# First image of a convolution-plus-attention kernel: diagonal products in short runs between the keys, mean products placed among them, the first norm summed by products, the vectors' transfers first

## The chip, the cores and the metric

The kernel runs on one core of a Trainium2 chip. Its time is the device time of one execution in microseconds. Before the change four runs took 3025.23, 3026.17, 3026.61 and 3026.94 us; the median is 3026.39 us. One further execution was profiled, and every time inside the kernel below is from that execution, counted from the start of its span. PE is the engine for matrix products, DVE the vector engine, ACT the scalar engine, POOL the GpSimd engine; SP only issues transfers.

## What is computed

The input is a batch of 4 images of 384 channels and 48 x 48 points, all float32. Cut to what matters:

```python
x_flat  = x.reshape(B, C, N).transpose(0, 2, 1)              # N = 2304 points
local   = depthwise_conv_7x7(x, conv_w) * inv + shift        # batch norm folded in
x_norm  = layernorm(x_flat, ln_gamma, ln_beta)               # over the 384 channels
q, k, v = split(x_norm @ qkv_w.T + qkv_b)                    # 8 heads of 48
q       = q + heads(layernorm(local_flat, ln_gamma, ln_beta))
out     = softmax(q @ k.T * 48 ** -0.5) @ v
y       = x_flat + out @ proj_w.T + proj_b
```

## The kernel before, in words

**Tiling.** An image is cut into 6 chunks of 8 image rows, 384 points each (`G`), numbered g; all images together have 24 chunks, numbered t. Channels lie on 128 partitions in `CC` = 3 groups c. Tensors come packed: group c holds two heads at partitions 0 and 64 and a third of the last two heads in the 16 partitions behind each, so a load of one tensor (`load_packed`) is four transfers.

**Per image.** `keys_values` (L423) makes keys and values of one chunk. It is a generator of three steps, each of six products of 128 x 128 by 128 x 384 (a float32 product shows in the profile as two instructions): value blocks 0 and 1; value block 2 and key group 0; key groups 1 and 2. ACT moves the results out of PSUM; for keys it adds `qkb`, the projection's bias joined with what the norm's beta gives (`shift_rows` makes that by products with beta, a row of 384 numbers for each of queries 0, keys 1 and values 2).

**Per chunk of queries** a pass of 12 slots follows (`NSLOT`). A slot makes six score tiles (L649), lets ACT take the exponential (L653), and weighs the values with the six tiles of the slot before (L664). Into these slots the rest is laid: the next chunk's 7 x 7 convolution, its norm, its query projection, the last chunk's output projection.

**The convolution.** One tap of one channel group is one DVE instruction (L240), 147 for a chunk. `conv_ops(t)` yields after each. A planner (L263 to L302) gives each half slot a weight and deals the 147 instructions of chunk t+1 over the half slots up to the first norm slot of chunk t (`norm_slots`, L281: 7 and 10 for t = 0). For the first chunk of all, ten of the 49 taps (`PE_TAPS`) go to PE instead, as products with diagonal matrices: ACT makes 30 diagonals (L250) from the identity and the taps, PE runs ten products per group (L256), and `add_products` adds the result to the DVE's accumulator.

**The norm.** In the first image DVE adds the three channel groups (`chunk_sum`, L313 and L314), PE spreads the mean over all partitions by one product with a constant matrix (`spread_mean`, L320), DVE subtracts it (`centre`, L324), ACT squares (L328), DVE sums, PE spreads again, ACT takes the inverse root in three instructions (L335 to L337), DVE corrects it (`newton`, L403 to L405) and multiplies (L738; for the convolution's result L531, in `query_end`). During the slots another form is used: `sum_out` sends the sums through DRAM, and `centre_by`, `variance`, `few_root` and `few_newton` finish on 12 columns.

**The first image's start** (L684 to L750) is an order written out by hand: PE, DVE and ACT run their instructions as written. So does SP in the section of loads (L117 to L196). After that section a scheduler places SP's and POOL's transfers among the others. The vectors are loaded as `norms` (batch norm and layer norm) and `taps_in`, scaled into `natural`, and sent piece by piece into the packed layout `vec` by 14 transfers (L162), by turns from ACT's and POOL's queues. `taps` and `diagonals` need `vec`. In the loads' section SP issues, after the vectors and the first slab (the 11 image rows that the first chunk's convolution reads): `w_v`, `staged[1]` (key weights), the chunk `xn` 1, `staged[0]` (query weights), chunks 2 to 5, `w_o`. The next slab's load belongs to the first convolution instruction and so comes behind them, and then the bias: `row` is written to DRAM (`bias<-row`, L709) and read back as `columns` (four transfers).

PSUM has one bank `m` for means, one bank `sums`, and three double banks `r` in a ring.

## Time and profile before

| | |
|---|---|
| median of 4 runs | 3026.39 us |
| profiled execution, its own time | 3026.74 us |
| its span | 3024.5 us |
| PE busy | 2980.4 us, 99% |
| DVE busy | 2305.5 us, 76% |
| ACT busy | 1560.8 us, 52% |
| first product of the whole run | 14.14 us |
| first scores of the first chunk (L649) | 151.23 us |
| first scores of the second chunk | 259.58 us |

The span is the profiled time from the first to the last instruction; 2.24 us of the execution's own time lie outside it. The slices of the page cut the span into 40 equal parts of 75.6 us, so the first image's start is the first two of them. A wait is shown in brackets with the instruction or transfer that ended it. The granted clock is 1.00 at full speed.

### The profile page before, as it was taken

The page shows a single profiled execution, that of the slowest core. Times are in us where ns is not written, and L with a number is a line of the kernel's source. Part 1 is how long each engine was busy: PE and PEld are TensorE (multiplying, and loading weights), DVE is VectorE, ACT ScalarE, POOL GpSimd, SP SyncE. Part 2 cuts the span into 40 slices and gives each one's busy share as a digit, 9 for nine tenths or more (in the row PEclk, how much of TensorE's full clock was granted, in tenths as well). Part 3 has the DMA queues.
Part 4 walks back from the last instruction along what each step waited for, and adds up shares of the span by engine and source line. Part 5 has one row for each costly group of instructions (what it writes and reads, how often), then busy time and mean ns, then how long its engine had stood idle before and what let it go on. Part 6 is the DMA issues. An engine that isn't in the chain of part 4 may idle for free.

```text
span 3024.5 us, 42309 instructions
## 1 busy us (share of the span) xinstructions
PE 2980.4 (99%) x15686; PEld 1357.6 (45%) x15686; DVE 2305.5 (76%) x4569; ACT 1560.8 (52%) x2385; POOL 19.0 (1%) x61
## 2 busy tenths in 40 slices
PE   6999999999999999999999999999999999999998
PEld 3544444444454444444455444444445444444443
DVE  6899989978765899888765888987876488788411
ACT  3354555555435555555534555555552555555553
POOL 1000000000000000000000000000000000000000
PEclk9999999999999999999999999999999999999999
DMA  6111111111101211111110111012010111100001
GB/s 115 25 25 28 34 34 34 31 39 37 27 25 30 47 33 30 36 30 38 29 33 23 33 39 42 22 34 48 25 28 24 27 27 33 25 27 19 17 26 29
DMA packets 98618, 98.89 MB, mean 33 GB/s; under 512 B 43617, under 2 KB 89185, under 8 KB 98402
## 3 DMA queue, kind: packets, MB, share of 16 engines
q1 hardware_dynamic: 97010, 95.42, 14.2%
q8 instruction: 125, 2.05, 0.3%
q10 hardware_dynamic: 752, 0.63, 0.1%
q14 instruction: 91, 0.75, 0.1%
q0 software_dynamic: 640, 0.05, 0.0%
HBM read 70.24 MB, written 15.25 MB: 28 GB/s over the span
## 4 chain that ended last, share of the span: by engine, by line
PE 93%; DVE 6%; DMA 0%; ACT 0%; issue 0%; SPq 0%; DVEq 0%; ACTq 0%
PE r L649 38%; PE o L664 37%; PE m L411 10%; PE r L411 8%; DVE acc L240 4%; DMA vec<-natural 0%; PE m L320 0%; PE r L256 0%; DVE sum L314 0%; PE o L256 0%; PE r L861 0%; DVE sum L313 0%; DVE xn L738 0%; DVE xn L324 0%; DMA taps_in<-in_conv_w_dram 0%
## 5 line engine op out<-in xcount | busy, mean ns | idle before, releaser
L653 ACT ACTIVATE pt<-r 128x768 f32<-128x768 f32 x1728 | 1276.6, 812 | 1168.0 <-PE o L664 738.2
L240 DVE SCALAR_TENSOR_TENSOR acc<-slab,vec,acc 128x368 f32<-128x368 f32 (+8 forms) x3429 | 1735.9, 583 | 7.7 <-DMA vec<-natural 7.7
L664 PE MATMUL o<-pt,v 128*49 128x384 f32 x6912 | 1173.8, 489 | 0.0
L649 PE MATMUL r<-q,k 48*128 48x384 f32 x5184 | 910.4, 497 | 4.1 <-DVE q L533 4.1
L664 PEld LDWEIGHTS o<-pt,v 128*49 128x49 f32 x6912 | 425.8, 124 | 709.0 <-issue 681.5
L649 PEld LDWEIGHTS r<-q,k 48*128 48x128 f32 x5184 | 441.1, 186 | 472.2 <-ACT pt L653 224.8
L649 PE MATMUL r<-qt,kt 48*128 48x384 f32 x1728 | 300.7, 493 | 1.3 <-ACT pt L653 1.3
L627 DVE SCALAR_TENSOR_TENSOR xr<-m,pb,xr 128x384 f32<-128x384 f32 x69 | 42.5, 615 | 281.8 <-PE m L411 281.8
L649 PEld LDWEIGHTS r<-qt,kt 48*128 48x128 f32 x1728 | 150.4, 185 | 151.3 <-ACT pt L653 69.1
L411 PE MATMUL m<-xn,w_qk 128*128 128x384 f32 x414 | 152.0, 503 | 0.0
L411 PE MATMUL m<-ao,w_o 128*128 128x384 f32 x414 | 152.0, 503 | 0.0
L411 PE MATMUL r<-xn,w_qk 128*128 128x384 f32 x450 | 149.3, 486 | 0.7 <-ACT q L525 0.7
L411 PE MATMUL r<-w_v,xn 128*128 128x384 f32 x432 | 147.3, 494 | 0.0
L313 DVE TENSOR_TENSOR sum<-sq 128x384 f32<-128x384 f32 x48 | 26.7, 555 | 113.2 <-ACT sq L328 113.1
L411 PEld LDWEIGHTS r<-xn,w_qk 128*128 128x128 f32 x450 | 85.4, 190 | 60.6 <-ACT q L525 1.3
L411 PEld LDWEIGHTS r<-w_v,xn 128*128 128x128 f32 x432 | 83.4, 194 | 60.0 <-issue 4.9
L411 PEld LDWEIGHTS m<-xn,w_qk 128*128 128x128 f32 x414 | 73.0, 189 | 74.2 <-issue 27.8
L411 PEld LDWEIGHTS m<-ao,w_o 128*128 128x128 f32 x414 | 73.0, 189 | 74.2 <-issue 14.2
L581 DVE RECIPROCAL rd<-rd 128x24 f32<-128x24 f32 (+2 forms) x25 | 7.5, 301 | 128.6 <-DMA rd<-den 128.6
L451 ACT COPY v<-r 128x384 f32<-128x384 f32 x72 | 32.2, 481 | 126.0 <-PE r L411 126.0
L447 ACT ACTIVATE k<-r,qkb 128x384 f32<-128x384 f32 x72 | 39.4, 581 | 68.4 <-PE r L411 68.4
L564 ACT COPY ao<-o 49x384 f32<-49x384 f32 x141 | 66.6, 473 | 1.7
(113 smaller groups left out, 813.8 us busy)
## 6 DMA issues: line engine op xcount, KB each, us to landing
xr<-in_x_dram SPq DMA_DIRECT2D x24, 576.0 KB
out_dram<-xr SPq DMA_DIRECT2D x72, 192.0 KB
slab<-in_x_dram SPq DMA_DIRECT2D x32, 378.0 KB
rb<-rden SPq DMA_DIRECT2D x48, 216.0 KB
xn<-in_x_dram SPq DMA_DIRECT2D x46, 216.0 KB
slab<-in_x_dram SPq DMA_DIRECT2D x16, 297.0 KB
slab<-in_x_dram SPq DMA_DIRECT2D x32, 126.0 KB
kt<-k SPq DMA_DIRECT2D x144, 24.0 KB
```

Of the source, the lines that this page charges most:

```text
L240: nc.vector.scalar_tensor_tensor(dst, src, weight, dst, ALU.mult, ALU.add)
L313: nc.vector.tensor_add(s, src[:, 0, :], src[:, 1, :])
L411: nc.tensor.matmul(dst, lhsT=weights(c), rhs=src(c), start=c == 0, stop=c == CC - 1)
L447: nc.scalar.activation(k[:, u, :], r[:, j, :G], AF.Identity, bias=qkb[:, 1, u : u + 1])
L451: nc.scalar.copy(v[:, u + NB, :, 0:HD], r[:, j, :C].rearrange("p (h d) -> p h d", d=HD))
L564: nc.scalar.copy(dst[r : r + HA], sums[r : r + HA, :G])
L581: nc.vector.reciprocal(rd, rd)
L627: nc.vector.scalar_tensor_tensor(xr[:, co, :], m, pb[:, co : co + 1], xr[:, co, :], ALU.add, ALU.add)
L649: nc.tensor.matmul(r[:, j, :G], lhsT=kk[:, blk * P : (blk + 1) * P], rhs=qq, start=True, stop=True)
L653: nc.scalar.activation(pt, r[:, :, :G], AF.Exp, scale=SCALE)
L664: nc.tensor.matmul(sums[r : r + HA, :G], lhsT=values[t // NG, kb // NB][:, kb % NB, 2 * p + j, :], rhs=pt[:, j, :], start=kb == 0, stop=kb ...
```

## The change

The change touches the start of the run, the first image's keys and values, and the pass of the very first chunk. The vectors: the layer-norm vector and the taps are issued from ACT, the first chunk of x from SP behind the slab, POOL makes its constants first, and POOL issues nine of the 14 transfers of `vec` and ACT five. POOL's instructions in the loads' section now run as written. The diagonals are made in four portions, and the 30 products run in portions of 3, 4, 3 and then 5, all into the bank `sums`. The sums over channels of the first chunk's norm are made by three products each (`spread_sum`). The rows of the bias go out in two parts: those of keys and values before the first keys, read back by `key_bias`, that of the queries later, read back by `query_bias`. In the loop over chunks the first step of the keys comes ahead of the next chunk's mean, and the taps are dealt anew (4, 4, 3, 8). In the very first pass the norm's slots are 8 and 10, and its norm uses `chunk_sum`, `spread_mean`, `centre` and `newton`.

```diff
-    def load_x(b, g, queue=nc.sync):
+    def load_x(b, g):
         t = big.tile([P, CC, G], F32, tag=f"xn{g}", name=f"xn{b}_{g}")
-        load_packed(t, x[b, :, g * G : (g + 1) * G], queue)
+        load_packed(t, x[b, :, g * G : (g + 1) * G])
         xn[b, g] = t
...
     loads = ExitStack()
-    loads.enter_context(tc.manual_schedule(engines={mybir.EngineType.SP}))
+    loads.enter_context(
+        tc.manual_schedule(engines={mybir.EngineType.SP, mybir.EngineType.Pool})
+    )
     nc.scalar.preload_act_table_set("natural_log_exp_and_others")
...
     nc.gpsimd.memset(neg_half, -0.5)
+    make_identity(nc, ident)
+    nc.gpsimd.memset(mean_w, 1.0 / C)
+    nc.gpsimd.memset(eps, LN_EPS)
     nc.sync.dma_start(out=norms[:, 0:4], in_=bn)
-    nc.sync.dma_start(out=norms[:, 4:6], in_=ln)
+    nc.scalar.dma_start(out=norms[:, 4:6], in_=ln)
     taps_in = big.tile([P, CC, T0], F32, tag="kt0", name="taps_in")
-    nc.sync.dma_start(out=taps_in, in_=conv_w)
+    nc.scalar.dma_start(out=taps_in, in_=conv_w)
     load_slab(0, 0)
-    load_x(0, 0, nc.scalar)
+    load_x(0, 0)
     nc.gpsimd.tensor_scalar_add(inv, norms[:, 3], BN_EPS)
     nc.gpsimd.tensor_tensor(inv, inv, neg_half, ALU.pow)
-    make_identity(nc, ident)
-    nc.gpsimd.memset(mean_w, 1.0 / C)
-    nc.gpsimd.memset(eps, LN_EPS)
     nc.vector.tensor_copy(natural[:, :, T0 + 1 :], norms[:, 4:6].rearrange("p v c -> p c v"))
...
         )
-    queues = cycle((nc.scalar, nc.gpsimd))
+    queues = cycle((nc.gpsimd, nc.scalar, nc.gpsimd))
     for c in range(CC):
...
-    def make_diagonals():
-        for c in range(CC):
-            for i, tap in enumerate(taps[:PE_TAPS]):
-                nc.scalar.mul(diagonal(c, i), ident, cw[:, c, tap : tap + 1])
+    def make_diagonals(c, first=0, end=PE_TAPS):
+        for i in range(first, end):
+            nc.scalar.mul(diagonal(c, i), ident, cw[:, c, taps[i] : taps[i] + 1])
+
+    coming_products = deque((c, i) for c in range(CC) for i in range(PE_TAPS))
+
+    def first_products(n):
-    def first_products(dst, c):
         slab, first, end = slabs[0, 0]
-        for i, tap in enumerate(taps[:PE_TAPS]):
-            src, part = window(slab, dst, 0, first, end, c, tap)
+        for _ in range(n):
+            c, i = coming_products.popleft()
+            src, part = window(slab, sums[:, :G], 0, first, end, c, taps[i])
             nc.tensor.matmul(
...
     def norm_slots(t):
-        return (6, 9) if t else (7, 10)
+        return (6, 9) if t else (8, 10)
...
+    def spread_sum(src):
+
+        m = bank()
+        project(m[:, :G], lambda c: mean_w, lambda c: src[:, c, :])
+        return m
+
     def centre(src, m):
...
-    bias = dram.tile([C, CC], F32, tag="bias", name="bias", bufs=1)
-
...
-    def copy_rows(some, row):
-        for i in some:
-            nc.scalar.copy(row[0:1, :, i], rows[i])
+    def rows_out(some):
+
+        row = work.tile([P, C, CC], F32, tag="rb", name="row", bufs=1)
+        row = row.rearrange("p c n -> p (c n)")[0:1, 0 : C * len(some)]
+        row = row.rearrange("o (c n) -> o c n", n=len(some))
+        for j, i in enumerate(some):
+            nc.scalar.copy(row[:, :, j], rows[i])
+        bias = dram.tile([C, len(some)], F32, tag=f"bias{some[0]}", name="bias", bufs=1)
+        columns = const.tile(
+            [P, CC, len(some)], F32, tag=f"columns{some[0]}", name=f"columns{some[0]}"
+        )
+        nc.sync.dma_start(out=bias.rearrange("(o c) i -> o c i", o=1), in_=row)
+        with nc.allow_non_contiguous_dma(reason="a few vectors, once"):
+            load_packed(columns, bias)
+        return columns
...
-    def bias_columns():
-        columns = const.tile([P, CC, 3], F32, tag="columns", name="columns")
-        with nc.allow_non_contiguous_dma(reason="a few vectors, once"):
-            load_packed(columns, bias)
-        for i in range(2):
-            nc.vector.tensor_add(qkb[:, i, :], qk_vec[:, i, :], columns[:, :, i])
+    def key_bias(columns):
+        nc.vector.tensor_add(qkb[:, 1, :], qk_vec[:, 1, :], columns[:, :, 0])
+        nc.vector.tensor_add(vbp, vbp, columns[:, :, 1:2])
+    def query_bias(columns):
+
+        nc.vector.tensor_add(qkb[:, 0, :], qk_vec[:, 0, :], columns[:, :, 0])
         nc.vector.tensor_add(qkb[:, 0, :], qkb[:, 0, :], beta)
-        nc.vector.tensor_add(vbp, vbp, columns[:, :, 2:3])
...
-    r = ring()
-    products = r[:, 0, :G], r[:, 1, :G], sums[:, :G]
-
     def add_products(c):
         a = accs[0][:, c, :]
-        nc.vector.scalar_tensor_tensor(a, products[c], shift[:, c : c + 1], a, ALU.add, ALU.add)
+        nc.vector.scalar_tensor_tensor(
+            a, sums[:, :G], shift[:, c : c + 1], a, ALU.add, ALU.add
+        )
-    make_diagonals()
-    first_products(products[0], 0)
-    convolve_first(16)
+    make_diagonals(0)
+    first_products(3)
+    convolve_first(2)
     src = xn[0, 0]
-    m = spread_mean(chunk_sum(src))
-    convolve_first(3)
+    m = spread_sum(src)
+    first_products(4)
+    convolve_first(4)
     centre(src, m)
-    row = work.tile([P, C, CC], F32, tag="rb", name="row", bufs=1)
-    shift_rows((2,))
-    first_products(products[1], 1)
     sq = squares(src)
-    copy_rows((2,), row)
-    scale_values()
-    convolve_first(6)
-    m = spread_mean(chunk_sum(sq))
+    make_diagonals(1, 0, PE_TAPS // 2)
+    convolve_first(4)
+    m = spread_sum(sq)
     root = inverse_root(m)
-    shift_rows((1, 0))
-    copy_rows((1, 0), row)
-    nc.sync.dma_start(out=bias.rearrange("(o c) i -> o c i", o=1), in_=row[0:1])
-    convolve_first(6)
+    shift_rows((2, 1))
+    first_products(3)
+    scale_values()
+    columns = rows_out((1, 2))
+    convolve_first(4)
     nc.vector.tensor_mul(src, src, over_chunks(newton(*root)))
+    make_diagonals(1, PE_TAPS // 2)
     for c in range(CC):
         scale_rows(1, c)
-    add_products(0)
-    add_products(1)
-    convolve_first(6)
-    s = chunk_sum(xn[0, 1])
     for g in range(NG):
+
+        last = g == NG - 1
+        src = accs[0] if last else xn[0, g + 1]
         making = keys_values(0, g)
-        src = xn[0, g + 1] if g + 1 < NG else accs[0]
+        next(making)
+        convolve_first(8 if last else 4)
+        if g % 2 == 0:
+            add_products(g // 2)
+        if g == 3:
+            query_bias(columns)
+        s = chunk_sum(src)
+        if g == 0:
+            key_bias(columns)
+        if last:
+            next(making)
         m = spread_mean(s)
+        convolve_first(4)
         centre(src, m)
         sq = squares(src)
-        next(making)
+        if not last:
+            next(making)
         convolve_first(3)
...
         root = inverse_root(m)
-        if g == 0:
-            bias_columns()
         next(making)
-        if g == NG - 1:
+        if g == 1:
+            shift_rows((0,))
+            columns = rows_out((0,))
+            make_diagonals(2)
+        if 0 < g <= CC:
+            scale_rows(0, g - 1)
+        if last:
             r, r2 = ring(), ring()
...
                 query_step(0, u, m)
-        convolve_first(7)
-        rs = newton(*root)
-        if g + 1 < NG:
-            nc.vector.tensor_mul(src, src, over_chunks(rs))
         else:
+            first_products(5 if g < 4 else 0)
+        convolve_first(8)
+        rs = newton(*root)
+        if last:
             query_end(0, rs)
-        next(making)
-        if g == 0:
-            first_products(products[2], 2)
-        if g < CC:
-            scale_rows(0, g)
-        convolve_first(6)
-        if g == 1:
-            add_products(2)
-        if g + 2 <= NG:
-            s = chunk_sum(xn[0, g + 2] if g + 2 < NG else accs[0])
+        else:
+            nc.vector.tensor_mul(src, src, over_chunks(rs))
...
             if s == second + 1 and following:
-                query_end(t + 1, few_newton(*root))
+                query_end(t + 1, few_newton(*root) if t else newton(*root))
             if s == X_SLOTS[0] + 1 and coming is not None:
...
                 sq = squares(accs[t + 1])
-            if (s == X_SLOTS[1] and coming is not None) or (s == second and following):
+            if (s == X_SLOTS[1] and coming is not None) or (s == second and following and t):
                 v = variance(sent.pop("x" if s == X_SLOTS[1] else "local"))
...
                 output_bias()
+            if t == 0 and s in (first, second):
+                m = spread_mean(sent.pop("local"))
             if s in OUT_SLOTS and t:
...
             if (s == X_SLOTS[1] and coming is not None) or (s == second and following):
-                root = few_root(v)
+                root = few_root(v) if t else inverse_root(m)
+            if s == first and t == 0:
+                centre(accs[1], m)
             convolve("slot", t, s, 1)
...
                 centre_by(coming, sent.pop("x"))
-            if s == first and following:
+            if s == first and following and t:
                 centre_by(accs[t + 1], sent.pop("local"))
...
             if s == first - 1 and following:
-                sent["local"] = sum_out(accs[t + 1])
+                sent["local"] = (sum_out if t else chunk_sum)(accs[t + 1])
             if s == X_SLOTS[0] + 1 and coming is not None:
...
             if s == first + 1 and following:
-                sent["local"] = sum_out(sq)
+                sent["local"] = (sum_out if t else chunk_sum)(sq)
```

## The prediction

> **What bounds the kernel now.** I read the page first, then PE's waits, then the chain, then the order in time up to 260 us.
>
> ```profile
> span 3024.5 us, 42309 instructions
> PE 2980.4 (99%) x15686; PEld 1357.6 (45%) x15686; DVE 2305.5 (76%) x4569; ACT 1560.8 (52%) x2385; POOL 19.0 (1%) x61
> PE   6999999999999999999999999999999999999998
> ```
>
> PE is the bound, except in the first slice. PE's waits from 148 us to the end (total, times, longest) and pieces of the chain that ended last (start, us) show the rest:
>
> ```profile
> PE r L649 <- DVE q L533: 4.1, 1, 4.1
> PE r L649 <- ACT pt L653: 1.3, 2, 1.0
> ```
>
> ```profile
> 148.70 40.82 DVE acc L240 x80
> 191.06 28.20 DVE acc L240 x55
> ...
> 259.58 6.51 PE r L649 x24
> ```
>
> After 259.58 PE never waits, so the end follows when the second chunk's scores start. That start is late for two reasons: the first scores begin only at 151.23, and in the first pass DVE is the chain and its query comes 4.13 us late, after which 24 products take 6.51 instead of 4.15 us at a halved clock (0.62 on average from 259.5 to 266). So PE effectively starts the second chunk at 259.58 + 2.36 = 261.94. I predict that point anew.
>
> The rows that decide, in order of time (start, length):
>
> ```profile
> 38.83 2.26 SPq L97 DMA_DIRECT2D slab<-in_x_dram  x4
> 43.71 0.28 SPq L709 DMA_DIRECT2D bias<-row  x1
> 44.04 0.41 SPq L613 DMA_DIRECT2D xr<-in_x_dram  x1
> 49.34 1.75 SPq L97 DMA_DIRECT2D columns<-bias  x4
> 54.65 0.23 DVE L497 TENSOR_TENSOR qkb<-qk_vec,columns 128x3 f32<-128x3 f32 x2
> ```
>
> ```profile
> 11.00:13.00 2.00, 0.00 (x0) 0.00 (x0) 0.00 (x0) 0.00 (x0) 0.89 (x2) 1.00 0.15 18
> 13.00:38.83 25.83, 20.90 (x50) 9.97 (x50) 18.75 (x36) 12.16 (x35) 5.91 (x17) 0.87 1.06 184
> 38.83:50.00 11.17, 5.00 (x15) 1.47 (x15) 8.08 (x14) 6.09 (x17) 0.00 (x0) 0.82 1.07 191
> 50.00:54.00 4.00, 4.00 (x10) 2.26 (x9) 3.17 (x5) 1.16 (x1) 0.00 (x0) 0.65 0.12 23
> ```
>
> A window shows its length, the busy time of PE, its weight loads, DVE, ACT and POOL, the granted clock, and last the transfers' busy share and GB/s. From 13 to 50 us the transfers are saturated by SP's loads, at 184 to 191 GB/s. The bias is written behind all of them and needs 5.6 us until SP may read it back (43.71 to 49.34). The load of `xr` belongs to the second pass and depends on nothing, yet was issued only after the bias: SP had no free moment before, so nothing overtook the loads.
>
> **The change, part by part.** *Key bias.* The new order has `key_bias` on DVE after only 18 taps and `add_products(0)`. DVE gets there near 33: vectors at 13.7, six taps to 18.5 (the third group's vector came at 16.89), mean product read at 20, `centre` 1.35, four taps, squares and mean product to 24.7, four taps, root to 26.4, `newton` and scaling 3.1, four taps 2, products' addition 0.6, sum 1.1. But SP still has to issue everything up to the slab first, whatever the row's readiness, and the bias still stands behind the slab's 1008 KB. So the columns come at a time L set by the loads. Before: last issue starts at 50.66; the batch-norm vector, issued 0.75 and used 3.00, gives 2.25 us, so L = 52.9; upper end 54.65, where DVE read them unhindered. The loads can gain what stood idle between 11 and 13 us (share 0.15), 0 to 2 us, since chunk 0 is now ahead of `w_v` on SP itself; I take 1.5: L = 51.4 (49.9 to 54.65). DVE then waits some 18 us. Behind it queue all taps, `centre` of chunk 1; behind those ACT's squares and key copies, then PE's next mean product.
>
> *Everything before this wait costs or gains nothing*, because DVE has 18 us to spare: the vectors' order (between 1.5 us gained and 1 us lost against 13.69, as POOL's issues take 5 us to land and stand behind slab and chunk; SP takes four loads of chunk 0 more, ACT three fewer; POOL's loads of `qk_vec` and `vbp` stand behind nine vector issues, needed at L only), the two `spread_sum` (8 instructions more on PE, 2.6 us; 2.2 us less on DVE), the portions of diagonals. If the cover went, they would count with these amounts, and the vectors most, since both PE and DVE start with them.
>
> *The loop after L*, each chunk by the engine that ends last (tap 0.48 us, 56.2 us by the first chunk's 117; a step of keys, 12 instructions, 3.87; warm mean product 0.81 and 0.95 until `centre`; five products 3.15; sum 1.12; root 1.75; `newton` 1.8; scaling 1.3). Chunk 0: bias, four taps, `centre`, three taps, sum: L+6.2; PE is cold, so mean product and step take 6.55 (49.15 to 55.71 before): L+12.75; five products: L+15.95. DVE has chunk 1 ready at L+13.2. Chunk 1: two steps, mean product, wait 0.3, mean product, step, query row 2.0, products: 18.35, to L+34.3. Chunks 2 and 3: 16.35 each, PE bound, to L+67.0. Chunk 4 has no products, PE is done at L+80.15, but DVE scales chunk 5 only at L+82.5 (19 taps, two sums, centre, newton, scaling, with the addition 16.35 a chunk). Chunk 5: two steps 7.7, of which 1.3 more at half clock (a wait of 2.06 brought that at 85.46), mean product; DVE ends the first chunk's taps, sums, `centre`s at L+92.5 and has the squares' sum at L+96.4; PE idles 4.2, then 6.55 cold and three query projections 5.85: L+108.85. So the first scores start at 160.25, 9.0 later than before. The 20 products moved behind L are in this sum; `query_bias` is hidden (its row goes out at L+32, two transfers of 5.6 and 4 us, needed at L+51.7).
>
> *The first pass.* PE had 104.22 us (151.23 to 255.45, 1.3 of it waits on ACT); two mean products add 1.6, and the waits on ACT end or stay: 104.5 to 105.8, I take 105.2. DVE: 132 taps at 0.537 (148.62 to 219.17 held 131 before), sum, then 47 taps of the next chunk instead of 59 ahead of the query, since the planner deals 147 over the longer way to slot 8; the small norm is replaced by `newton` and saves 2.8 us. DVE starts 1.2 us after PE and has the query at 104 of PE's 105.2; both new PE waits (slots 8 and 10) are met within 0.5 us. So the 4.13 and 2.36 go, which is gain 5.5 less 1.6 and noise. The 12 taps moved on (6.2 us at 0.515, 26.80 by 52) are hidden by the second pass, whose query stood ready 14 us early (357.46 against 372.2).
>
> *Sum:* 160.25 + 105.2 = 265.45 against 261.94: 3.5 us more. Profiled execution 3026.74 + 3.5 = 3030.2; it stands 0.35 above the median, so 3029.9.
>
> Two rules of the Trainium skill, set beside these rows. By "TensorE: Matmul & The Clock Gate", section "Why this matters for your kernels", PE loses its clock after idle gaps above about 3 us. The rule speaks against breaking up the products. The trace is stricter: 2.06 us of waiting sufficed for 0.50 from 87.0 to 90.2. By the page the wait of 2.35 before chunk 5 would be free and the sum 2.2 us; by the row it is 3.5. By "DMA: Bandwidth & Descriptors", section "Issuing engines are not separate DMA queues", spreading transfers over queues saves issue time only; by that the vectors' reordering would be worth at most ACT's three issues, about 1.3 us, and nothing under the wait.
>
> **Rivals.** *A, the columns come early.* If the scheduler puts the bias between the loads as soon as its row exists (30), it lands 5.6 later, the read-back 5 to 6 after: L = 42, the pass starts at 150.85, and the time is 3020.5; with no wait at all PE is bound from 30.5 on and it is 3010. For it speaks that rows go out in two parts; against it the place of `xr`. *B, slower: the columns come later still.* If `xr` (576 KB) is issued ahead of the bias, 3.2 us at 184 GB/s come on top: L = 54.6, 3033.1. It decides from L = 54 on. The scheduler's order is not shown; speaking for it, 0.33 us lay between the two issues; against it, the row is ready earlier now. *C, DVE again sets the second chunk.* Its query has 1.2 us to spare; at 0.56 instead of 0.537 us a tap 179 taps end 4.1 later, PE waits 2.9 and pays 2.36 at half clock again: 3035. For it speaks that DVE is the chain there now, against it the 12 taps and 2.8 us that go. *D, the reordered vectors come no earlier:* 0 us, under the wait.
>
> **How the numbers follow.** Forecast 0.60, A 0.13, B and C together 0.20, others 0.07 (4 slower, 3 same). 0.2% is 6.05 us, about what a measurement tells from no change: 3020.3 to 3032.4. A lies beyond the lower bound in 0.12. The forecast spreads 3.5 us by L (3028.4 to 3033.2) and clock, so 0.08 of its 0.60 lies above, and with 0.14 of B and C and 0.04 others slower is 0.26; same 0.62. The range 3020 to 3036 leaves out most of A's 0.13 and the worst 0.06.
>
> **What would show it.** DVE idle some 18 us before the bias additions, ended by `columns`; PE idle beside it and cold after; first scores near 160; second chunk's scores without a DVE wait, clock 1.00. I am wrong if the bias is written before 38, or if the chunks' periods after L differ from 16 to 18 us.

## The result

The changed kernel takes 3029.96 us (median of 32 runs, 3026.37 to 3037.44) against 3026.04 us of the kernel before (52 runs beside them, 3024.61 to 3028.04). The ratio is 1.0013, with a 95% interval of 1.0008 to 1.0018: 3.9 us slower, which is less than 0.2%, but an unchanged time lies outside the interval. The forecast was 3029.9. The profiled execution of the changed kernel took 3033.53 us (span 3031.7), 3.57 more than its median; where that lies is shown below.

The page's first lines and TensorE's row of the 40 slices, for the changed kernel:

```profile
span 3031.7 us, 42328 instructions
PE 2983.3 (98%) x15698; PEld 1360.0 (45%) x15698; DVE 2300.6 (76%) x4556; ACT 1560.5 (51%) x2385; POOL 19.9 (1%) x63
PE   5999999999999999999999999999999999999998
```

PE is the bound as before, and the first slice has got emptier, not fuller. The first slice is where the order changed. These are the rows of the changed kernel, in order of time (start, length; what ended the idle time before it), that answer to the rows of the bias in the prediction:

```profile
38.09 2.40 SPq L97 DMA_DIRECT2D slab<-in_x_dram  x4
41.29 0.29 SPq L496 DMA_DIRECT2D bias<-row  x1
41.71 0.42 SPq L633 DMA_DIRECT2D xr<-in_x_dram  x1
49.12 1.75 SPq L97 DMA_DIRECT2D columns<-bias  x4
```

```profile
26.78 0.90 ACT L491 COPY row<-r 1x384 f32<-1x384 f32 x2 [0.69 <-PE r L422]
52.24 0.16 DVE L514 TENSOR_TENSOR qkb<-qk_vec,columns 128x3 f32<-128x3 f32 x1 [20.86 <-DMA columns<-bias]
```

SP issues the bias at 41.29, behind the second slab, although ACT had the row ready at 27.7. The columns can be read at L = 52.24, and DVE, which was there at 31.4, stands for 20.86 us.

The windows of the changed kernel over the same stretches as before (length, busy time of PE, its weight loads, DVE, ACT and POOL, the granted clock, the transfers' share and GB/s):

```profile
11.00:13.00 2.00, 1.71 (x3) 1.11 (x4) 0.49 (x1) 2.00 (x8) 1.98 (x5) 1.00 0.93 187
13.00:38.83 25.83, 23.89 (x68) 11.81 (x67) 14.57 (x25) 13.03 (x36) 5.19 (x10) 1.00 1.09 174
38.83:50.00 11.17, 0.00 (x0) 0.00 (x0) 0.00 (x0) 0.00 (x0) 0.00 (x0) 0.57 1.07 189
50.00:54.00 4.00, 0.00 (x0) 0.00 (x0) 1.71 (x5) 0.00 (x0) 0.00 (x0) 0.50 0.11 20
```

PE works more than before until 38.83 (23.89 us against 20.90), and then none of the core's engines works for eleven microseconds, only the transfers run. The hole in the transfers at 11 to 13 us is gone (187 GB/s against 18), and yet the stream after it was slower in this execution (174 GB/s against 184).

PE's waits of the changed kernel, first from 8 to 300 us and then, in the second fence, from 148 us to the end (total, times, longest):

```profile
PE m L325 <- DVE sum L319: 26.0, 4, 21.4
PE o L261 <- ACT pt L251: 11.3, 1, 11.3
PE r L422 <- ACT k L458: 1.8, 1, 1.8
```

```profile
PE m L325 <- DVE sum L319: 4.2, 1, 4.2
PE r L422 <- ACT q L545: 0.7, 1, 0.7
PE m L422 <- DVE ao L868: 0.4, 1, 0.4
```

The wait of 4.13 us for the second chunk's query, which set the kernel before, is in neither. The wait of 21.4 behind DVE's wait has come. The last rows that carry the reading are PE's around the first scores, and where the first pass ends:

```profile
148.29 0.88 PE L325 MATMUL m<-sum,mean_w 128*128 128x384 f32 x2 [4.16 <-DVE sum L319]
149.01 7.66 PE L422 MATMUL r<-xn,w_qk 128*128 128x384 f32 x18
157.35 4.14 PE L422 MATMUL r<-xn,w_qk 128*128 128x384 f32 x12 [0.67 <-ACT q L545]
161.42 4.15 PE L669 MATMUL r<-q,k 48*128 48x384 f32 x24
...
268.52 4.15 PE L669 MATMUL r<-q,k 48*128 48x384 f32 x24
```

The first scores start at 161.42, which is 10.2 later than before and L + 109.18. The second chunk's scores start at 268.52 at full clock. That is 6.6 later than the 261.94 that stood for the kernel before, and as much as the profiled execution is longer (6.79). Of these 6.6 us, 3.42 belong to this execution: the clock fell to 0.50 inside the first pass, while PE was never idle (windows of the changed kernel, same columns):

```profile
186.00:190.00 4.00, 4.00 (x26) 1.73 (x22) 4.00 (x9) 2.61 (x5) 0.00 (x0) 1.00 0.50 103
193.92:200.75 6.83, 6.83 (x25) 2.90 (x26) 6.83 (x15) 2.43 (x3) 0.00 (x0) 0.50 0.00 1
200.75:210.00 9.25, 9.25 (x56) 3.81 (x54) 9.25 (x19) 5.25 (x8) 0.00 (x0) 1.00 0.01 2
```

Half of 6.83 us is 3.42. Without it the first pass is 107.10 - 3.42 = 103.68 us long, as in the experiments (103.76 to 103.9), and the execution would have taken 3030.1, the median.

### The profile page after: what moved, and what is told of

It is laid out like the page before. It is cut to its first block, busy times and chain, and to the rows that moved or that the text cites. A ratio compares the mean times of both kernels' runs of the same rounds, so it can differ in the third digit from the quotient of the medians.

```text
span 3031.7 us, 42328 instructions
## 1 busy us (share of the span) xinstructions
PE 2983.3 (98%) x15698; PEld 1360.0 (45%) x15698; DVE 2300.6 (76%) x4556; ACT 1560.5 (51%) x2385; POOL 19.9 (1%) x63
## 3 DMA queue, kind: packets, MB, share of 16 engines
HBM read 70.19 MB, written 15.24 MB: 28 GB/s over the span
## 4 chain that ended last, share of the span: by engine, by line
PE 95%; DVE 3%; DMA 2%; ACT 0%; issue 0%; SPq 0%; DVEq 0%; ACTq 0%
PE r L669 38%; PE o L684 37%; PE m L422 10%; PE r L422 9%; DVE acc L242 2%; DMA xn<-in_x_dram 1%; PE o L261 0%; PE m L325 0%; DMA bias<-row 0%; DMA w_o<-in_proj_wT_dram 0%; PE r L890 0%; DMA taps_in<-in_conv_w_dram 0%; DMA w_v<-in_qkv_wT_dram 0%; DVE xn L335 0%; DMA vec<-natural 0%
## 5 line engine op out<-in xcount | busy, mean ns | idle before, releaser
L422 PEld LDWEIGHTS m<-ao,w_o 128*128 128x128 f32 x414 | 73.0, 189 | 74.6 <-issue 13.6
```

Source lines behind the costliest of these rows:

```text
L422: nc.tensor.matmul(dst, lhsT=weights(c), rhs=src(c), start=c == 0, stop=c == CC - 1)
```

## The experiments

The theory is the prediction's: the loop over the chunks starts when the columns land, each microsecond of L is one of the end, and the first pass is a gain of its own that the columns' wait eats up. The rivals are that the columns don't bind, that the first pass is no gain, and that the loop's new order itself is what costs. Every edit is against the changed kernel unless it says otherwise, and the time of the kernel before on the same chip is given where it matters (3026.2 to 3026.4).

### What sets the start of the loop

**The bias on POOL's queue.**

```
-        nc.sync.dma_start(out=bias.rearrange("(o c) i -> o c i", o=1), in_=row)
+        nc.gpsimd.dma_start(out=bias.rearrange("(o c) i -> o c i", o=1), in_=row)
...
-            load_packed(columns, bias)
+            load_packed(columns, bias, nc.gpsimd)
```

> The changed kernel, with the bias rows written and read back by POOL's queue instead of SP's, so that they no longer stand behind SP's issues; the loads stay as they are. My theory: the wait for the columns sets the start of the loop, and each microsecond of it is one of the end. The row is written by ACT at 27.7; with the loads saturating the transfers, a small transfer took 4 to 5 us to land (the vectors issued at 3.2 to 6.9 began at 8.5 to 10), so the write is done near 32.5 and the columns land at L = 38 (37 to 42) instead of 52.2. DVE waits 6.5 us instead of 20.9, and the time is 3030.0 - 14.2 = 3015.8 (to 3019.8). Rival: the small transfers stand behind all that SP has issued, whatever queue they are issued on; then L is 50 or more and the time 3028 or more. Second rival: the start of the loop isn't the bound, and L falls while the time stays within 3 us of 3030.

Measured: 3022.26 us (11 runs; against before 0.9987, interval 0.9978 to 0.9996), 7.7 less than the changed kernel. In order of time, for this kernel:

```profile
27.70 0.52 POOL L496 DMA_DIRECT2D bias<-row  x1 [7.96 <-ACT row L491]
35.52 2.22 POOL L97 DMA_DIRECT2D columns<-bias  x4 [7.30 <-DMA bias<-row]
```

```profile
44.83 0.16 DVE L514 TENSOR_TENSOR qkb<-qk_vec,columns 128x3 f32<-128x3 f32 x1 [13.71 <-DMA columns<-bias]
```

The issue no longer waits for SP, but the transfer still stands in the stream: the write took 7.8 us from issue to its use, the read-back 9.3. So L is 44.8, not 38. The median moved by 7.7 and L, in the one profiled execution of each, by 7.4: the slope is near one, and the columns are what binds. The size of L was the miss, since I had taken the landing times of the vectors, which go out when the stream has just begun.

**The loads behind the bias.**

```
-    for g in range(2, NG):
-        load_x(0, g)
...
-    load_packed(w_o, proj_wT)
     loads.close()
...
-        if t + 1 < NT:
+        if t and t + 1 < NT:
             load_slab(*divmod(t + 1, NG))
...
     columns = rows_out((1, 2))
+    later = ExitStack()
+    later.enter_context(tc.manual_schedule(engines={mybir.EngineType.SP}))
+    for g in range(2, NG):
+        load_x(0, g)
+    load_packed(w_o, proj_wT)
+    load_slab(0, 1)
+    later.close()
```

> The changed kernel, with the loads of chunks 2 to 5, of the output weights and of the second slab moved on SP behind the first bias rows. My theory: the bias is late only because these loads stand ahead of it. 3.9 MB are loaded ahead of it now, so at 187 GB/s the stream is empty near 28, the bias is issued at 28 and its columns land at L = 34 (33 to 37); DVE, there at 31.4, waits 2.6 us instead of 20.9, PE stays warm or nearly, and the time is 3030.0 - 18.2 = 3011.8, down to 3010 if PE keeps its clock. Rival: the chunks loaded later now come late themselves (chunk 2 is needed near 51, chunk 3 near 67); then PE or DVE waits for xn and the time stands above 3016. Second rival: the end isn't set by the columns and the time stays near 3030.

Measured: 3007.36 us (5 runs, 3007.03 to 3010.55; against before 0.9939, interval 0.9925 to 0.9952). In order of time, for this kernel:

```profile
27.85 0.28 SPq L493 DMA_DIRECT2D bias<-row  x1
28.18 0.33 SPq L97 DMA_DIRECT2D xn<-in_x_dram  x1
29.07 1.74 SPq L97 DMA_DIRECT2D columns<-bias  x4
```

```profile
32.18 0.16 DVE L511 TENSOR_TENSOR qkb<-qk_vec,columns 128x3 f32<-128x3 f32 x1 [0.64 <-DMA columns<-bias]
```

With the stream drained, the write needs 1.2 us and the read-back 3.1. The columns come 20.06 us earlier, the first scores 23.01 (138.41), and the time is 22.6 less. What goes beyond the columns fits PE's clock: it never falls before 125 us here, while in the changed kernel it stood at 0.50 from 40.3 to 64.2, where PE worked 5.75 us, and half of that is 2.9. No chunk comes late (no wait of PE or DVE for a chunk after the first). The time is 2.6 us better than the prediction's "no wait at all".

**The residual's load ahead of the bias, and then behind the columns.** The first is the prediction's slower rival, made on purpose.

```
     load_packed(w_o, proj_wT)
+    first_xr = work.tile([P, CC, G], F32, tag="xr", name="xr0", bufs=1)
+    nc.sync.dma_start(out=first_xr, in_=x[0, :, 0:G].rearrange("(c p) n -> p c n", p=P))
     loads.close()
...
-    residuals = {}
+    residuals = {0: first_xr}
...
-                if t:
+                if t > 1:
                     load_residual(t - 1)
```

> The changed kernel, with the load of the second pass's residual (576 KB) issued ahead of the second slab and of the bias. It is the slower rival of the prediction, made on purpose, and a measure of the slope. Theory: every transfer ahead of the bias is paid in full at the end: 3.1 us more at 184 to 187 GB/s, L = 55.3, 3033.1. Rival: it is hidden (the second chunk or DVE sets the end, or the transfers have room): 3030.0, or under half of 3.1.

Measured: 3030.12 us (11 runs, 3028.64 to 3035.06), 0.2 more than the changed kernel, not 3.1. Its profiled execution has the bias issued at 40.04, the read-back at 48.51, and L = 51.66. That asks where the 576 KB went. The second run holds the same load back:

```
             key_bias(columns)
+            first_xr = work.tile([P, CC, G], F32, tag="xr", name="xr0", bufs=1)
+            nc.vector.memset(first_xr[:, 0, 0:1], 0.0)
+            nc.sync.dma_start(out=first_xr, in_=x[0, :, 0:G].rearrange("(c p) n -> p c n", p=P))
+            residuals[0] = first_xr
...
-                if t:
+                if t > 1:
                     load_residual(t - 1)
```

> The changed kernel, with the load of the second pass's residual (576 KB, issued at 41.71 right behind the bias) held back until DVE has added the key bias; a one-element memset on DVE does that. With this load put ahead of the bias the time did not move (3030.12 against 3029.96), against the 3.1 us that the slower rival had given it. Theory: since in the changed kernel it stands ahead of the columns' read-back (issued at 49.12, landed at 52.24) all the same, so its 3.1 us are in the forecast's time already; held back, the columns land near 49 and the time is 3026.9 (3026 to 3028). Rival: the read-back waits for the slab alone and the residual's load costs nothing in either place: L near 52 and 3029 to 3031.

Measured: 3029.59 us (11 runs, 3025.32 to 3031.88). My theory falls, the rival stands: L is 51.75 with the load gone from the stream. In order of time, and the windows of that kernel:

```profile
40.96 0.29 SPq L496 DMA_DIRECT2D bias<-row  x1
48.65 1.75 SPq L97 DMA_DIRECT2D columns<-bias  x4
52.15 0.41 SPq L748 DMA_DIRECT2D xr<-in_x_dram  x1
```

```profile
44.00:48.00 4.00, 0.00 (x0) 0.00 (x0) 0.00 (x0) 0.00 (x0) 0.00 (x0) 0.50 0.92 136
48.00:52.00 4.00, 0.00 (x0) 0.00 (x0) 0.21 (x2) 0.00 (x0) 0.00 (x0) 0.50 0.06 1
```

From 48 us the transfers are idle, and the read-back takes its 3.1 us all the same. So the read-back, 3.12 us in the changed kernel with the end of the residual's load beside it and 3.10 here without, is not held by that load (in the full stream, on POOL's queue, it took 9.3). What holds L is the write, 7.7 us behind the slab. Why the same load ahead of the write did not delay it either is only in part accounted for: from 13 to 40 us that profiled execution loaded at 187 GB/s, the changed kernel's at 175, which makes 324 KB of the 576. The rest stays open.

The profiles show one more thing. Five kernels with the changed kernel's loop write the bias on SP behind the same loads (one of them behind the residual's too). They have L from 50.48 to 54.57, which goes mostly with the rate at which the loads came in, and the first scores follow L (the sixth row is the kernel with the bias on POOL's queue):

| kernel | GB/s from 13 to 40 us | L | first scores | difference |
|---|---|---|---|---|
| first pass's part undone | 189 | 50.48 | 160.37 | 109.89 |
| residual ahead | 187 | 51.66 | 160.25 | 108.59 |
| residual held back | 177 | 51.75 | 160.94 | 109.19 |
| changed kernel | 175 | 52.24 | 161.42 | 109.18 |
| output bias moved | 164 | 54.57 | 163.79 | 109.22 |
| bias on POOL's queue | 164 | 44.83 | 154.64 | 109.81 |

The two rows near 109.85 are those in which the clock lost 3.4 us around the squares' sum; in the others it lost 1.7. So in these profiles the rate of the loads reaches the first scores through L. Its runs spread over 11 us where those of before spread over 3.4, which this may explain; only one execution of each kernel has a trace.

**The additions of the key bias later on DVE**, the columns as late as ever.

```
-        if g == 0:
-            key_bias(columns)
         if last:
             next(making)
...
-        if not last:
+        if 0 < g < NG - 1:
             next(making)
...
         root = inverse_root(m)
+        if g == 0:
+            key_bias(columns)
+            next(making)
         next(making)
```

> The changed kernel, with only the place of the two additions of the key bias moved: behind the root of chunk 1, as the kernel before has them, with the keys' copies of chunk 0 that need them. The loads stay, so the columns land at 52.2 as before. Theory: the price of the wait is what stands behind it on DVE. Here 15 taps, the centring, the two sums of chunk 1 and its two mean products and PE's products of chunk 0 are done ahead of it, so DVE has chunk 1 scaled at L + 7 and PE's first step of chunk 1 starts at 59 to 60 instead of 69.05: 9 us less, 3021 (3019.5 to 3023). Rival: the landing of the columns alone sets the end, since the keys can't be written without them: within 2 us of 3030.

Measured: 3022.64 us (11 runs; against before 0.9991, interval 0.9982 to 1.0000), 7.3 less than the changed kernel with the same L:

```profile
36.26 0.56 DVE L319 TENSOR_TENSOR sum<-sum,sq 128x384 f32<-128x384 f32 x1
52.24 0.16 DVE L514 TENSOR_TENSOR qkb<-qk_vec,columns 128x3 f32<-128x3 f32 x1 [15.43 <-DMA columns<-bias]
...
58.30 1.36 DVE L776 TENSOR_TENSOR xn<-xn,y 128x1152 f32<-128x1152 f32 x1
```

```profile
46.83 3.31 PE L261 MATMUL o<-slab,pt 128*128 128x384 f32 x10
59.75 6.06 PE L422 MATMUL r<-w_v,xn 128*128 128x384 f32 x12 [9.62 <-issue]
```

DVE (first fence) now does chunk 1's centring and sums ahead of its wait, and PE (second fence) the two mean products, chunk 0's keys and five diagonal products, so PE's first step of chunk 1 starts at 59.75 (expected 59 to 60) instead of 69.05. The profile calls PE's 9.62 us before it "issue"; they end as DVE has scaled chunk 1 (58.30 and 1.36). So of what the late columns cost, a part is not their lateness but what was queued behind the two small additions and the step of keys that needs them.

### What each part is worth

**The first pass's part alone, in the kernel before** (the norm slots and the product sums of the first chunk's pass, as in the change).

```
     def norm_slots(t):
-        return (6, 9) if t else (7, 10)
+        return (6, 9) if t else (8, 10)
...
-                sent["local"] = sum_out(sq)
+                sent["local"] = (sum_out if t else chunk_sum)(sq)
```

> The kernel before, with only the first pass's part of the change: the mean and the mean of squares of the second chunk's convolution by products of TensorE in slots 8 and 10 instead of the small norm in 7 and 10, and so 12 taps moved into the second pass. My theory: this part alone is a gain; the wait of PE for the second chunk's query (4.13 us) and the halved clock after it (2.36) go, two mean products cost 1.6, so 4 to 5 us less: 3021.5 (3021 to 3023). Rival: the first pass is not better by it (DVE late at slots 8 or 10, or a drop of the clock in the pass as the changed kernel's profile shows at 193.9 to 200.8): within 2 us of 3026.

Measured: 3019.89 us (11 runs, 3019.36 to 3023.26; 0.9981, interval 0.9972 to 0.9990), 6.5 less than before. Its first pass goes from 150.39 to 254.29, without a wait for the query, 103.9 us long.

**The same part undone in the changed kernel**, the edit the other way round.

```
     def norm_slots(t):
-        return (6, 9) if t else (8, 10)
+        return (6, 9) if t else (7, 10)
...
-                sent["local"] = (sum_out if t else chunk_sum)(sq)
+                sent["local"] = sum_out(sq)
```

> The changed kernel, with the first pass's part undone: the small norm in slots 7 and 10 again, 59 taps ahead of the query. Theory: it is an independent gain, which the columns' wait eats up: 6.5 us as in the kernel before with this part alone, so 3036.5 (3035 to 3037.5). Rival: with DVE's taps moved behind the wait the first pass depends on it more, so undoing it costs 8 us or more: 3038 and above; or, PE starting later against DVE, less than 4: below 3034.

Measured: 3037.34 us (5 runs, 3035.82 to 3039.94; 1.0039, interval 1.0026 to 1.0053), 7.4 more than the changed kernel. The wait for the query is back (its waits of PE from 148 us on):

```profile
PE r L669 <- DVE q L553: 3.9, 1, 3.9
PE r L669 <- ACT pt L673: 1.6, 1, 1.6
```

Both ways the part is worth about 7 us (6.5 and 7.4), with the loop's start at 54.6 in the one and 50.5 in the other.

**The vectors' part alone, in the kernel before.**

```
...
-    nc.sync.dma_start(out=norms[:, 4:6], in_=ln)
+    nc.scalar.dma_start(out=norms[:, 4:6], in_=ln)
...
-    nc.sync.dma_start(out=taps_in, in_=conv_w)
+    nc.scalar.dma_start(out=taps_in, in_=conv_w)
...
-    load_x(0, 0, nc.scalar)
+    load_x(0, 0)
...
-    queues = cycle((nc.scalar, nc.gpsimd))
+    queues = cycle((nc.gpsimd, nc.scalar, nc.gpsimd))
```

> The kernel before, with only the transfers' part of the change: vectors' transfers first, spread over POOL and ACT, the first chunk's load on SP, POOL's order written out. My theory: the vectors come 2.85 us earlier (first product at 11.3 instead of 14.1, as the changed kernel shows), and here no wait lies on top of it until the columns are read; those come 1.5 us earlier (the loads fill the hole at 11 to 13 us). So the time is 1.5 to 2.9 us less: 3023.9 (3023.1 to 3024.6). Rival: nothing is gained since the columns come no earlier and DVE, 1.7 us after them in the kernel before, now waits: 3024.3 to 3026.

Measured: 3025.16 us (11 runs, 3023.34 to 3026.27), 1.2 less, with an interval (0.9985 to 1.0003) that takes in no change. By itself it settles neither theory. The profiled execution took 3023.34 us, the least of the eleven; in it the first scores start at 148.63, 2.60 earlier than before, and DVE reads the columns at 52.51, 2.14 earlier. So in that execution the part gave what the theory says, and in the median it did not.

**The vectors' part undone where nothing covers it**: the kernel with the loads behind the bias, and the edit above the other way round.

```
...
-    nc.scalar.dma_start(out=taps_in, in_=conv_w)
+    nc.sync.dma_start(out=taps_in, in_=conv_w)
...
-    load_x(0, 0)
+    load_x(0, 0, nc.scalar)
...
-    queues = cycle((nc.gpsimd, nc.scalar, nc.gpsimd))
+    queues = cycle((nc.scalar, nc.gpsimd))
```

> The changed kernel with the loads moved behind the bias (which ran in 3007.4 and left DVE a wait of 0.6 us for the columns), and in it the vectors' part undone: their transfers in the old order on the old queues. Theory: in the changed kernel the earlier vectors (2.85 us) are worth nothing only because the wait for the columns covers them; without the cover they count in full, 2.85 us later: 3010.2 (3009.3 to 3011). Rival: they are worth what the kernel before showed, 1.2 us, or nothing, the loads being the bound of the start: 3007.4 to 3008.6.

Measured: 3008.45 us (5 runs, 3007.93 to 3010.38), 1.1 more. The five runs overlap with the five of the new order (3007.03 to 3010.55), so 1.1 us stands for little or nothing: the rival fits better than the theory's 2.85. The first product starts at 13.76 here and at 12.04 with the new order, so between these two executions the vectors come 1.7 earlier, not 2.85, and the first scores 1.56 earlier (138.41 against 139.97). The rule that the prediction weighed, the Trainium skill's "DMA: Bandwidth & Descriptors", section "Issuing engines are not separate DMA queues", says that more queues save the issue time alone. The estimate of 1.3 us made from it is near both medians, and below the shift of the first scores in both pairs of profiles (2.60 and 1.56).

**The old order of the first image, with the other two parts and early columns.** Against the kernel before: the two edits above, and the loads moved behind the columns' read-back.

```
         if g == 0:
             bias_columns()
+            later = ExitStack()
+            later.enter_context(tc.manual_schedule(engines={mybir.EngineType.SP}))
+            for gx in range(2, NG):
+                load_x(0, gx)
+            load_packed(w_o, proj_wT)
+            load_slab(0, 1)
+            later.close()
```

> The kernel before with three things: the first pass's part, the vectors' part, and the loads of chunks 3 to 5, of the output weights and of the second slab behind the columns' read-back. So it is the changed kernel with the loads moved (3007.4), less the new order of the first image. Theory: in the old order DVE was itself only ready to read the columns at 54.65, so their coming early gives 0 to 1.5 us on top of the two parts' 6.5 and 1.2: 3017.8 (3017 to 3018.6), and the new order is worth 10 us once the columns are early, though it costs 11 when they are late. Rival: the old order gains from early columns too, DVE standing for other reasons; then it comes to 3007 to 3011, and the order is worth little.

Measured: 3018.82 us (10 runs, 3016.87 to 3020.50; 0.9974, interval 0.9964 to 0.9983). That is what the two parts give by themselves (3026.3 - 6.5 - 1.2 = 3018.6), so early columns give the old order nothing, since DVE reads them without waiting:

```profile
42.65 1.75 SPq L97 DMA_DIRECT2D columns<-bias  x4
52.41 0.23 DVE L496 TENSOR_TENSOR qkb<-qk_vec,columns 128x3 f32<-128x3 f32 x2
```

(Chunk 2's load still goes out at 21.00 in this kernel, ahead of the bias; from 31 us on the transfers are idle, and the bias goes out at 41.38, when ACT has the last row.) The new order of the first image therefore adds 11.4 us with the columns late (3018.6, which is the sum above and not a run, to 3030.0) and takes 11.5 off with the columns early (3018.8 to 3007.4, two runs). The order is good; whether the bias stands behind the loads decides its sign.

### The clock, and a better kernel

**The output bias's products moved out of the first pass**, into the gap in which PE waits for the squares' sum.

```
     def output_bias():

-        m = bank()
+        m = ring()[:, 0]
...
         convolve_first(3)
+        if last:
+            output_bias()
...
-            if t == 0 and s == CC:
-                output_bias()
```

> The changed kernel, with the 18 one-column products of the output's bias moved out of the first pass (slot 3) into the 4.2 us in which PE idles in the last chunk, ahead of the mean of squares. They hold PE for 2.17 to 2.50 us. In the changed kernel's profiled execution the clock fell to 0.50 from 193.9 to 200.8, right after them, though PE never idled; in the kernel with the vectors' part alone it fell right after them too, from 182 to 187; in the three other profiles it did not. Theory: these products, narrow as they are, count as rest for the clock, and in a part of the executions cost 1.7 to 3.4 us more than their own time; then the median falls by 3.5 to 5 us, to 3025.0 to 3026.5, the slowest runs fall more than the fastest, and no drop of the clock shows in the first pass. Rival: the drop is chance; then only their own 2.2 us go, less 0 to 0.7 for DVE's addition in the chain: 3027.8 to 3028.4, with the same spread.

Measured: 3027.95 us (11 runs, 3026.58 to 3030.76), 2.0 less: about the products' own time, as the rival has it, though the intervals of the two kernels' ratios overlap. The spread didn't shrink in a way that these runs could tell. So what happened in the changed kernel's profile at 193.9 is not a usual cost of the kernel. It isn't chance alone either: of twelve profiles with these products in the pass, three show a drop there, and each of the three begins within the products or less than 1.3 us behind them (193.92 in the changed kernel, where they lie from 192.26 to 194.76; 182.9 in the kernel before with the vectors' part alone and in the old order with early columns, where they end at 181.7). From 300 to 2990 us, in windows of 5 us, the clock stays at 1.00 in all fourteen profiles. What picks the three is left open.

**The loads behind the bias, and the last chunk rearranged.**

```
...
-        if last:
-            next(making)
+        if last:
+            added = output_bias()
         m = spread_mean(s)
         convolve_first(4)
         centre(src, m)
         sq = squares(src)
-        if not last:
-            next(making)
-        convolve_first(3)
+        next(making)
+        convolve_first(2 if last else 3)
...
-        convolve_first(8)
+        convolve_first(5 if last else 8)
...
-            query_end(0, rs)
+            query_end(0, rs, 4)
+            nc.vector.tensor_add(pb, pb, added[:, 0:CC])
...
-            if t == 0 and s == CC:
-                output_bias()
```

(`query_end` runs the four taps between its scaling and the query's additions.)

> The changed kernel with the loads behind the bias, and in the last chunk of the loop: the output bias's 18 products in the gap ahead of the first mean product, one step of keys ahead of the mean product and two behind it instead of two ahead and one behind, nine of the fifteen taps moved behind the sums. In the kernel with the loads moved alone PE idled 0.7 there for the query, 4.16 for the squares' sum (a halved clock behind it cost 1.7 more) and had 2.2 us of the 18 products in the first pass. Theory: the first scores start at 134.0 instead of 138.4 and the first pass is 2.2 shorter, 6.6 us less: 3000.8 (3000 to 3002.5). Rival: DVE, which had the second chunk's query only 1.1 us ahead of PE there, is now late for it; PE waits 1 to 3 us at the second chunk and loses 1.7 to 3.4 by the clock: 3003 to 3006.

Measured: 3001.85 us (5 runs, 3001.51 to 3003.26; 0.9921, interval 0.9908 to 0.9935), 24 us less than before, and 5.5 less than with the loads moved alone (6.6 expected; the parts of the rearrangement were not run one by one). PE around the first scores in this kernel:

```profile
116.02 2.06 PE L419 MATMUL r<-vbp,w_o 128*128 128x1 f32 x18
117.95 0.89 PE L322 MATMUL m<-sum,mean_w 128*128 128x384 f32 x2
118.68 2.10 PE L419 MATMUL r<-w_v,xn 128*128 128x384 f32 x6
120.61 2.10 PE L419 MATMUL r<-xn,w_qk 128*128 128x384 f32 x6
122.76 0.88 PE L322 MATMUL m<-sum,mean_w 128*128 128x384 f32 x2
123.48 5.97 PE L419 MATMUL r<-xn,w_qk 128*128 128x384 f32 x18
130.12 4.14 PE L419 MATMUL r<-xn,w_qk 128*128 128x384 f32 x12 [0.67 <-ACT q L542]
134.19 4.32 PE L668 MATMUL r<-q,k 48*128 48x384 f32 x24
```

The gap of 4.16 is gone, the clock shows no drop from 8 to 300 us, the first scores start at 134.19 (expected 134.0), and the second chunk's at 236.02 without a wait. The rival, DVE late for the second chunk, did not come.

## Why the prediction was right

**The number.** 3029.9 was forecast, 3029.96 measured. In the forecast's own terms: first scores 9.0 later, against 10.2 in the profile; first pass 5.5 shorter, against 7.0 (110.7 with the wait and the halved clock before, 103.7 now); sum 3.5, against 3.2 by the profile without the drop at 193.9 and 3.9 by the medians. Two terms were off by 1.2 and 1.5 in opposite directions, so that the sum fits to 0.1 us is luck.

**Key bias and L.** "DVE gets there near 33" was 31.4; "L = 51.4 (49.9 to 54.65)" was 52.24 there and 50.48 to 54.57 over the executions; "DVE then waits some 18 us" was 20.86. The mechanism stands: the loads set L, not the row's readiness. The 1.5 us that I gave to the filled hole came (187 GB/s in it), and a slower stream took as much back: 10 GB/s less over 25.83 us is 258 KB, 1.5 us at 174 GB/s.

**The loop after L.** L + 108.85 was forecast, L + 108.59 to 109.89 measured on the five other rows of the table and 109.18 here. Chunk 1 started at L + 16.8 (15.95), chunk 2 at L + 35.2 (34.3), and the next ones 16.55, 16.28 and 15.24 after each other (16.35, 16.35, 15.5). The gap of 4.2 us before the squares' sum is in the profile as 4.16. Here too errors cancelled: the 1.3 us for a halved clock in chunk 5 did not come, while chunk 0 took 0.85 more than I gave it and the products behind the gap 13.1 instead of 12.4 (148.29 to 161.42). The test named in the prediction, periods of 16 to 18 us, was badly put: chunks 1 and 4 are outside by their own terms (18.35 and 15.5), and by the profile too.

**The first pass, mis-sized.** I took 105.2 us, from a range of 104.5 to 105.8; it is 103.7 to 103.9. The waits on ACT (1.3 us), which I let "end or stay", ended. Another 0.8 us went, and 0.7 of it is in the score products of the last three slots: these 72 take 13.3 us before, where the two waits cut runs of 24 into twice 12, and 12.6 now. DVE was in time, both new waits of PE (slots 8 and 10) are absent from the list of waits, and the gain of the part, 6.5 alone and 7.4 undone, is larger than the 5.5 in the sum.

**"Everything before this wait costs or gains nothing"** is not contradicted: DVE stood 20.86 us in front of the additions. The first product starts 1.7 to 3.3 us earlier, more than my bound of 1.5, and without the cover this is worth 1.1 to 1.2 us in the median, at the edge of what the runs tell. No run undid the vectors' part under the cover, so that it is worth nothing there is read from DVE's wait and not measured.

**The rivals.** A, columns early: its price was about right as a slope (44.83 gave 3022.3, where it asks for 3023.3), and "no wait at all, 3010" was 3007.4. B, the residual ahead: its mechanism was made and costs 0.2, not 3.2, so the order of these two transfers could not have decided anything; L above 54 was seen once, with a stream of 164 GB/s. C, DVE setting the second chunk: not seen in any run with the new norm. D, the vectors no earlier: false by the first product (11.29 against 14.14), and without weight, as said.

**The clock.** The prediction held a wait of 2.06 us enough for a halved clock, against the rule of the Trainium skill's "TensorE: Matmul & The Clock Gate", section "Why this matters for your kernels", with its gaps of about 3 us. The runs show no sharp length at all. PE's gap of 2.06 us (the old order has it) lost 1.71 us in three profiles and nothing in a fourth, one of 1.65 lost 1.71 in the kernel with the old norm, those of 1.81 lost nothing in any of ten, and those of 4.16 lost 1.7 or 3.4. Two gaps of 1.77 and 1.83, 0.9 us apart (from 22.8 to 27.28 in the kernel before with the first pass's part), were followed by 0.50 until past 32 us. So the wait that I priced by the row ("1.3 more at half clock") was right to be a chance and wrong to be a fixed price: the changed kernel's 1.81 there cost nothing. And a gap isn't needed, as the window from 193.92 shows.

## What to carry to other kernels

When work is moved ahead, look at the oldest thing that each of its inputs stands behind: here a row of 3 KB was ready at 27.7 and waited 13.6 us for SP to issue loads of which nothing was read before 67 (chunk 2's sum, at 67.09), and the same order of work was worth 11 us more or 11 us less by that. A wait costs what is queued behind it on its engine, so place a wait for a late input behind everything that doesn't need it (7.3 us here, for moving two additions of 0.16 us and the step of keys that needs them). Find the stretch in which one wait covers others before pricing a part: the vectors' part gave about 1 us where no such wait lay on top, and nothing was to be expected of it where DVE stood still for 20.86 us behind it.

## What was not expected of the hardware

- A small transfer issued into a saturated stream takes as long to land from POOL's queue (7.8 us for the write, 9.3 for the read-back) as from SP's (7.8 for the write); with the stream drained the same write takes 1.2 and the read-back 3.1.
- The rate of the same loads differs between executions, 164 to 189 GB/s from 13 to 40 us.
- A gap of PE costs clock in some executions and not in others (2.06 us: 1.71 lost three times of four).
- The granted clock fell to 0.50 for 6.83 us with PE busy all the time, in or just after 18 products of one column each (2.17 to 2.50 us of PE). Three profiles of twelve show a fall there, of 1.71 or 3.42 us.
- 576 KB loaded ahead of the bias, or held back until its read-back had landed, made no difference to the time above 0.4 us.
